# Batch 0's gate and up products as seven block products, and the weight sums for them spread over two slots

## The chip, the cores and the metric

The kernel runs on one core of one Trainium2 chip, in one launch. The metric is the device time of that launch in microseconds. Everything is float32. TensorE (PE) multiplies matrices into PSUM, VectorE (DVE), ScalarE (ACT) and GpSimd (POOL) work elementwise, and SyncE (SP) issues nearly all of the transfers, one after the other in program order; each engine likewise takes its own instructions in program order.

## The reference

One layer of a transformer: attention with a residual, then a gated feed-forward network with a residual, on four batches of 512 tokens of 512 features.

```python
B, T, D, FF = 4, 512, 512, 1376          # 32 heads of 16, 8 key/value heads

def attention(x):                         # x: layernorm of the input
    q, k, v = x @ Wq, x @ Wk, x @ Wv      # heads of 16; q and k are rotated (rope)
    att = einsum('bhgqd,bhkd->bhgqk', q, k) / sqrt(16)
    probs = softmax(where(causal, att, -inf))
    return (probs @ v) @ Wo

def ffn(x):                               # x: layernorm of the sum so far
    up = x @ W_up.T                       # 512 -> 1376
    gate = silu(x @ W_gate.T)             # 512 -> 1376
    return (gate * up) @ W_down.T         # 1376 -> 512

x = x + attention(layernorm(x))
x = x + ffn(layernorm(x))
```

## The kernel before

**Slots.** Attention goes by groups: a batch has eight, each with four of the 32 heads. A call of slot(b) works off the eight groups of batch b, and weaves other PE work between their scores as filler: a list of steps, each with a planned cost in microseconds. After each of the four score visits of a group, and in slots 1 to 3 after its averages too, gap(n) issues filler until a planned share of the slot's total is done. So the order on each engine is written out by the program and fixed. Slot 0 weaves in the projections (queries, keys, values) of batches 1 to 3; slot 1 the rest of batch 3's queries, batch 0's output projection, its second layernorm, all its gate and up products, the last 96 features (edge) and half of its down product; slots 2 and 3 the same kind of work for batches 1 and 2, and batch 3's feed-forward network comes after the last slot. By the planned costs slot 1 holds 123.0 us of filler and slot 2 117.8.

**A group on the engines.** PE makes scores in two orientations (L993, L1006) into two pairs of banks. DVE reads one for the row maxima (L1039), ACT takes the exponentials of the other (L1094) into tiles e0, e1 and e2, POOL masks these (L1099), and PE averages the values with them (L1121). At a group's end POOL also makes a masked copy of the queries for a later group (masked, L978); SP stores the maxima (lowest, L1080) and lays them into those query tiles (L1089, L1091) a group ahead. DVE transposes the averages (L1135), takes the reciprocal (L1138), and POOL scales them (L1145). While slot 0 runs, POOL also does half of the rotation of queries and keys (L359, L363) and spreads the keys (L425).

**Gate and up, two ways.** For batch 0, ordinary(n) takes ten blocks of 128 features, for each a gate half and an up half of four products over 512 tokens. Each product is issued as four column tiles of 32 (L299, while narrow is set), and the trace has two records of each tile. The weights of a block come by load_f from the inputs, two blocks ahead, into the tile shared. For batches 1 to 3, seven(b, n, blocks) takes ten units, each the gate or the up part of 256 features, as a 2x2 block product with seven multiplications instead of eight (Winograd's form). Its steps are a1, y1, y2, v1, v2, w1 and w2, each with two products over 256 tokens. DVE joins them (L738, L748, L749, L757), ACT copies one of them into the tail of the rotation table (once, L727), and POOL multiplies gate and up in slots 2 and 3 (L721). It reads four sums of the activations (sums_of, on DVE, L682), which lie in xnTs[1] under the name turn, and weight blocks that load_blocks brings from DRAM (packed, L675), about a unit ahead, in four kinds of places in the tile shared.

**The weight sums.** Of a unit's seven weight blocks, three are plain copies from DRAM to DRAM (copies, L653 and L654, issued in slot 0), and four are sums that POOL makes (packs, L640): two loads of 256 KB into half of a spare tile, four adds of 128x256, one store of 512 KB (L643). Before the change this spare tile is xnTs[1], and all ten units are made in slot 1, woven in by timed at planned times 8.2 us apart. Batch 0 cannot use them, and does not.

**Other queues.** The output weights (wo_sb) are loaded at the very start. The list idle holds POOL work that pool_steps issues a few at a time in each gap; before the change it is empty in slots 0 and 1. A load whose place was just stored from waits on SP until the store has landed, and whatever SP has to issue after it waits too.

Of the kernel before, what the change touches and what calls it, by code (L numbers as in the profile page):

```python
# [74 lines left out]
def preln_block_kernel(  # L75
# [87 lines left out]
    whole = NF - 1  # L163
    packed = [dram.tile([P, 7, 2 * P], F32, name=f"packed{u}") for u in range(whole)]
    turn = xnTs[1].rearrange("p k t -> p (k t)")
    sums = turn.rearrange("p (s k t) -> p s k t", s=4, k=2)
    spare = turn.rearrange("p (u f m) -> p u f m", u=2, f=4)
    rest_w = rope_sb[:, : 2 * NK * 96].rearrange("p (a k m) -> p a k m", a=2, k=NK)


# [4 lines left out]
    def load_w(t, src):  # L175
        nc.sync.dma_start(out=t, in_=src.rearrange("(k p) m -> p k m", p=P))
# [105 lines left out]
    idle = deque()  # L282

    def pool_steps(n):
        for _ in range(min(n, len(idle))):
            idle.popleft()[1]()

    def need(tag):
        while any(t == tag for t, _ in idle):
            pool_steps(1)  # L290
# [328 lines left out]
    def after(step):  # L619
        return 0.0, step  # L620

    def packs(u):


        w, at = (wg, wu)[u % 2], 2 * P * (u // 2)
        t = spare[:, u % 2]

        def load():
            for i in range(2):
                load_w(t[:, 2 * i : 2 * i + 2, :].rearrange("p f (k m) -> p (f k) m", k=2), w[:, at + P - P * i :][:, :P])  # L630

        def combine(n):
            a11, a12, a21, a22 = (t[:, f, :] for f in range(4))
            out_, one, two, op = (
                (a22, a21, a22, ALU.add),
                (a21, a11, a21, ALU.subtract),
                (a11, a22, a11, ALU.subtract),
                (a12, a12, a11, ALU.subtract),
            )[n]
            nc.gpsimd.tensor_tensor(out_, one, two, op)  # L640

        def store():
            nc.sync.dma_start(out=packed[u][:, 3:, :], in_=t)  # L643

        return load, combine, store
# [22 lines left out]
        )  # L668

    def load_blocks(kind, v):  # L670
        if v >= (B - 1) * whole:
            return
        blocks = places[kind][1]
        src = packed[v % whole][:, blocks[0] : blocks[-1] + 1 : max(blocks[-1] - blocks[0], 1), :]
        nc.sync.dma_start(out=place(kind, v).rearrange("p f k m -> p f (k m)"), in_=src)  # L675
# [8 lines left out]
    def seven(b, n, blocks):  # L684
# [16 lines left out]
            return t.rearrange("p (h t) -> p h t", h=2)  # L701

        def unit(u):
            v, a, f = (b - 1) * whole + u, u % 2, 2 * (u // 2)
            left, right = slice(0, 2 * P), slice(2 * P, T)
            out = (u_sb if a else home[:, f : f + 2, :]).rearrange("p f t -> p (f t)")
            corners = out.rearrange("p (h t) -> p h t", h=4)[:, 0:4:3, :]
            ps = {}

            def twice(t):  # L710
                return t.unsqueeze(1).broadcast_to([P, 2, 2 * P])

            def ended():
                for which in (1, 0):
                    g, t = home[:, f + which, :], u_sb[:, which, :]
                    if a == 0:
                        nc.scalar.activation(t, g, AF.Tanh, scale=0.5)
                        carried.append(lambda g=g, t=t: nc.vector.scalar_tensor_tensor(g, t, 1.0, g, ALU.add, ALU.mult))
                    else:
                        engine = nc.gpsimd if narrow[0] else nc.vector  # L720
                        engine.tensor_tensor(g, g, t, ALU.mult)  # L721

            def a1():
                load_blocks("y", v + 1)
                ps["a"] = bank()
                product(ps["a"][:, left], 1, place("a", v)[:, 0])
                nc.scalar.copy(once, ps["a"][:, left])  # L727

            def y1():
                load_blocks("v", v + 1)  # L730
                load_blocks("a", v + 1)
                ps["y"] = bank()
                product(ps["y"][:, left], 2, place("y", v)[:, 0])
                owed()

            def y2():
                product(ps["y"][:, right], 6, place("y", v)[:, 1])
                nc.vector.tensor_tensor(halved(out[:, T:]), halved(ps["y"]), twice(once), ALU.add)  # L738

            def v1():  # L740
                load_blocks("w", v + 1)
                ps["v"] = bank()
                product(ps["v"][:, left], 7, place("v", v)[:, 0])
                owed()

            def v2():
                product(ps["v"][:, right], 5, place("v", v)[:, 1])
                nc.vector.tensor_tensor(corners, halved(ps["v"]), twice(out[:, 3 * T // 2 :]), ALU.add)  # L748
                nc.vector.tensor_tensor(out[:, right], ps["v"][:, right], out[:, left], ALU.add)  # L749

            def w1():
                ps["w"] = bank()
                product(ps["w"][:, left], 4, place("w", v)[:, 0])

            def w2():
                product(ps["w"][:, right], 3, place("w", v)[:, 1])
                nc.vector.tensor_tensor(corners, halved(ps["w"]), corners, ALU.add)  # L757
                ended()

            return [(0.86, step) for step in (a1, y1, y2, v1, v2, w1, w2)]  # L760

        steps = []
        for u in range(whole):
            steps += unit(u)
            if u % 2:
                steps.append(after(lambda p=u // 2: later_sums(b, n, p, (0, 1))))
        t = [after(lambda s=s: sums_of(s)) for s in range(4)]
        ends = edge(n)
        steps[12:12] = [after(moved)]
        for cut, step in zip((44, 50, 56, 62, 66, 72), blocks):  # L770
            steps.insert(cut, after(step))
# [407 lines left out]
    begin1[1]()  # L1179
    load_w(wv_sb, wv)  # L1180
    load_columns(wq_sb, wq, P, D)
    load_w(wo_sb, wo)
    thin[0] = False
    for cost, step in turned:
        step()
# [53 lines left out]
    def slot(b, steps):  # L1239
# [19 lines left out]
        def gap(n):  # L1259
            nonlocal done, part  # L1260
            part += total * shares[n] / 8
            pool_steps((3, 2, 2, 0, 3)[n])
            done = fill(steps, part, done)

        for g in groups:
# [48 lines left out]
    early = [*rest1[16:-8], *turns, begin3, *rest2, *turned3, *rest3[:-24]]  # L1314
    for u in range(whole):
        early.insert(4 * u + 4, after(lambda u=u: copies(u)))
    slot(0, early)

    before, behind = attended(0, by_pe=(2, 3))
    tiles = list(down(0, 0))  # L1320
# [13 lines left out]
        assert not asides  # L1334
        return out_steps

    asides = []
    for u in range(whole):
        load, combine, store = packs(u)
        at = 8.2 * u + 6.0  # L1340
        asides += [(max(at - 9.9, 0.5), load), (at + 5.0, store)]
        asides += [(at + 1.0 * n, lambda n=n, combine=combine: combine(n)) for n in range(4)]
    asides += [(6.0, spilled), (34.0, load_down), (34.1, load_rest)]
    start1 = [
        before[0],
        *rest3[-24:-12],
        *before[1:],
        after(lambda: load_f(0)),
        *rest3[-12:-1],
        *behind,  # L1350
        rest3[-1],
        after(lambda: load_f(1)),
    ]
    blocks = [after(lambda kind=kind: load_blocks(kind, 0)) for kind in "ayvw"]
    layer = [*ordinary(0), *edge(0), *tiles[:5], *blocks, *tiles[5:cut]]
    slot(1, [*start1, *timed(layer, asides)])

    def split(b, n):

# [65 lines left out]
```

## Time and profile before

| | |
|---|---|
| time, median of 3 runs | 847.11 us (846.38 to 848.0) |
| the profiled execution | 848.06 us |
| its span, first to last instruction | 845.8 us |
| PE busy | 822.5 us, 97% |
| DVE busy | 545.5 us, 65% |
| POOL busy | 352.5 us, 42% |
| ACT busy | 231.3 us, 27% |
| moved by DMA | 101.57 MB, mean 120 GB/s |
| granted TensorE clock | 1.00 |
| stretch before slot 0 | 0 to 49.8 us |
| stretch after slot 3 | 705.0 to 845.8 us |

The times are from the first to the last instruction of the span. Busy times are unions: two matmuls that run side by side on different tiles of the array count once. A group of instructions has one line: source line, engine, operation, output and inputs by name, shapes, count, then its busy time, the mean of one, and the idle time of the engine just before its instructions with what ended most of it. Matmul ends are modelled, so a busy PE may still wait a little inside.

By the chain that ended last, PE is 76% of the span, DVE 12%, POOL 4% and DMA 3%. The filler's matmuls (L299 and L296) are 52% of it and the scores L993 12%.

### The profile page before, as it was taken

Reading aid. Unit: us, or ns where it says so; the run is one execution under the profiler, and the core shown is the slowest. Engines: PE = TensorE matmul, PEld = TensorE weight load, DVE = VectorE, ACT = ScalarE, POOL = GpSimd, SP = SyncE. Lnnn points to the kernel's source line nnn. Section 1 sums busy time; section 2 is a strip of 40 time slices with the busy share of each in tenths; the row PEclk is TensorE's granted clock in tenths of the full one; section 3 lists DMA queues with packets and bytes.
Section 4 is the critical chain, followed back from the end, with each engine's and each line's share of the span. In section 5 each row is a group of like instructions: output and inputs, shape, how many; then the busy total and the mean of one; then the engine's idle time right before and its main releaser. Section 6 shows DMA issues by size and latency. Waiting matters only on the chain.

```text
span 845.8 us, 28256 instructions
## 1 busy us (share of the span) xinstructions
PE 822.5 (97%) x11980; PEld 452.2 (53%) x11980; DVE 545.5 (65%) x1601; ACT 231.3 (27%) x342; POOL 352.5 (42%) x514
## 2 busy tenths in 40 slices
PE   6999999999999999999999999999999999999998
PEld 5654444544333335333555555436655556788887
DVE  7877777778555554458677776686877633656632
ACT  1045654422232322222233232222323331011100
POOL 4575574773544344223265634532244444101130
PEclk9999999999999999999999999999999999999999
DMA  8533304003764742253344632325333534545811
GB/s 259 124 96 78 91 16 91 5 3 64 232 191 144 235 137 77 88 200 77 84 155 140 196 115 66 115 47 151 96 97 103 162 106 148 119 146 174 291 33 50
DMA packets 149517, 101.57 MB, mean 120 GB/s; under 512 B 59696, under 2 KB 137264, under 8 KB 149136
## 3 DMA queue, kind: packets, MB, share of 16 engines
q1 hardware_dynamic: 149104, 94.01, 38.3%
q10 hardware_dynamic: 288, 5.77, 1.8%
q8 instruction: 94, 1.54, 0.8%
q14 instruction: 31, 0.25, 0.1%
HBM read 78.32 MB, written 25.17 MB: 122 GB/s over the span
## 4 chain that ended last, share of the span: by engine, by line
PE 76%; DVE 12%; POOL 4%; DMA 3%; issue 2%; ACT 1%; SPq 1%; POOLq 0%; DVEq 0%; ACTq 0%
PE mm L299 38%; PE mm L296 14%; PE sc L993 12%; DVE junk L1039 6%; PE av L1121 6%; PE sc L1006 4%; PE mm L590 2%; POOL e L1099 1%; DMA shared<-packed 1%; PE mm L582 1%; DVE st L218 1%; DVE rot L358 1%; ACT e L1094 1%; POOL home L425 1%; POOL qa L978 1%
## 5 line engine op out<-in xcount | busy, mean ns | idle before, releaser
L1039 DVE CUSTOM_DVE_ANT_0 junk<-sc,mask 128x128 f32<-128x128 f32 (+3 forms) x512 | 251.2, 491 | 139.0 <-PE sc L1006 78.4
L1094 ACT ACTIVATE e<-sc 128x1024 f32<-128x1024 f32 (+1 forms) x192 | 165.5, 882 | 384.4 <-PE sc L1006 300.7
L299 PE MATMUL mm<-xnT,shared 128*32 128x256 f32 (+1 forms) x3520 | 244.2, 420 | 2.3 <-DMA shared<-in_wg 1.5
L1099 POOL TENSOR_SCALAR_AFFINE_SELECT e<-e 128x512 f32<-128x512 f32 (+2 forms) x192 | 105.7, 560 | 225.4 <-ACT e L1094 222.3
L299 PEld LDWEIGHTS mm<-xnT,shared 128*32 128x32 f32 x3520 | 116.9, 110 | 113.0 <-issue 62.8
L993 PE MATMUL sc<-home,qa 32*64 32x512 f32 (+6 forms) x2048 | 156.1, 421 | 6.5 <-DVE low L1039 3.0
L1006 PE MATMUL sc<-qa,home 32*64 32x512 f32 (+6 forms) x2048 | 152.2, 427 | 1.5 <-DVE low L1039 0.8
L993 PEld LDWEIGHTS sc<-home,qa 32*64 32x64 f32 x2048 | 66.8, 131 | 90.2 <-DVE low L1039 29.1
L1121 PE MATMUL av<-e,home 128*32 128x512 f32 (+3 forms) x1024 | 81.9, 438 | 1.8 <-POOL e L1099 1.6
L296 PE MATMUL mm<-xnT,shared 128*128 128x256 f32 x360 | 80.3, 383 | 1.0 <-DMA shared<-packed 1.0
L296 PEld LDWEIGHTS mm<-xnT,shared 128*128 128x128 f32 x360 | 68.3, 192 | 12.8 <-issue 2.2
L299 PE MATMUL mm<-wd_sb,home 128*32 128x256 f32 (+3 forms) x848 | 71.4, 470 | 0.0
L1006 PEld LDWEIGHTS sc<-qa,home 32*64 32x64 f32 x2048 | 58.8, 130 | 22.5 <-issue 8.7
L1121 PEld LDWEIGHTS av<-e,home 128*32 128x32 f32 x1024 | 30.5, 109 | 47.2 <-issue 35.0
L299 PEld LDWEIGHTS mm<-wd_sb,home 128*32 128x32 f32 (+1 forms) x848 | 28.2, 110 | 36.9 <-issue 28.2
L299 PE MATMUL mm<-wo_sb,cx 128*32 128x512 f32 x384 | 45.4, 595 | 0.0
L797 POOL TENSOR_TENSOR wd_sb<-home 128x256 f32<-128x256 f32 x15 | 11.4, 759 | 75.6 <-DVE home L721 75.3
L1039 DVE DVE_READ_ACCUMULATOR2_ANT low<- 128x1 f32 x512 | 42.4, 83 | 0.0
L221 POOL TENSOR_TENSOR rstd<-rstd,neghalf 128x1 f32<-128x1 f32 x24 | 16.0, 667 | 56.8 <-DVE rstd L220 56.7
L1145 POOL TENSOR_TENSOR inv<-us,inverse 128x256 f32<-128x256 f32 x32 | 20.9, 654 | 44.5 <-DVE inverse L1138 44.3
L359 POOL TENSOR_TENSOR rot<-rot,rope_sb 128x512 f32<-128x512 f32 x18 | 25.7, 1425 | 23.0 <-DVE rot L358 22.8
L721 POOL TENSOR_TENSOR home<-home,u 128x512 f32<-128x512 f32 x20 | 25.2, 1281 | 21.2 <-DVE u L757 21.2
(146 smaller groups left out, 855.6 us busy)
## 6 DMA issues: line engine op xcount, KB each, us to landing
shared<-packed SPq DMA_DIRECT2D x90, 256.0 KB
flip<-u SPq DMA_DIRECT2D x88, 64.0 KB
packed<-xnT SPq DMA_DIRECT2D x10, 512.0 KB
xnT<-flip SPq DMA_DIRECT2D x18, 256.0 KB
wd_sb<-differences SPq DMA_DIRECT2D x7, 640.0 KB
shared<-packed SPq DMA_DIRECT2D x30, 128.0 KB
rows<-in_x SPq DMA_DIRECT2D x14, 256.0 KB
out<-rows SPq DMA_DIRECT2D x13, 256.0 KB
```

Of the source, the lines that this page charges most:

```text
L296: nc.tensor.matmul(out, lhsT=lhsT, rhs=rhs, start=start, stop=stop)
L299: nc.tensor.matmul(out[c : c + 32], lhsT=lhsT[:, c : c + 32], rhs=rhs, start=start, stop=stop)
L359: put(lambda: engine.tensor_tensor(rot, rot, sin, ALU.mult))
L590: nc.tensor.matmul(ps[96:P, ts(q, P)], lhsT=rest_w[:, a, kq, 32 * q : 32 * q + 32], rhs=xnTs[0][:, kq, most:], start=kq == 0, stop=kq == N ...
L721: engine.tensor_tensor(g, g, t, ALU.mult)
L993: nc.tensor.matmul(dst[at : at + 64, :n], lhsT=qa[g][rows_of(r), q : q + 64], rhs=keys_of(g)[rows_of(r), :n], start=True, stop=True,)
L1006: nc.tensor.matmul(dst[at : at + 64, first_q:], lhsT=keys_of(g)[rows_of(r), k : k + 64], rhs=qa[g][rows_of(r), P * j + first_q :], start=True,
L1039: nc.vector.tensor_tensor_reduce(out=junk[:, :n], in0=src, in1=mask[:, T - n : T] if i else mask[:, T:], scale=-1.0, scalar=BIG, op0=ALU.a ...
L1094: nc.scalar.activation(dst, src, AF.Exp, scale=1.0 / math.sqrt(DH))
L1099: nc.gpsimd.affine_select(out=e[rows, heads, c : c + P], in_=e[rows, heads, c : c + P], compare_op=ALU.is_ge, fill=0.0, base=base, pattern ...
L1121: nc.tensor.matmul(av[32 * r : 32 * r + 32, P * j :], lhsT=v[:, j, 4 * (m // 2) + r, DH * (1 - hf) : DH * (3 - hf)], rhs=e[:, r, c : c + n ...
L1145: nc.gpsimd.tensor_tensor(us[m][:, :, hf, :], turned[0][:, :, hf, :], by, ALU.mult)
```

## The change

Four things change together. (1) Batch 0's gate and up products go through seven instead of ordinary; its four activation sums stand at the head of its list, two before the steps a1 and y1 and two behind them, the edge comes at the end, and no sums for a seven-product down projection are queued. (2) The weight sums are made earlier: units 0 to 4 in slot 0, with the tile of the output weights as their spare, and units 5 to 9 in slot 1, with home tile 0's blocks 6 to 9 as theirs, which hold batch 0's keys and values until slot 0 ends and hidden features of batch 0 from unit 6 on. (3) They go through idle: one sum in each of the first three gaps of a group in slot 0, five a group in slot 1; a load or store that stands at the head of the list is issued along with them. (4) The output weights are loaded when slot 0's steps are done and the last sum is stored. The first blocks of kinds a and y are loaded at the start of slot 1, v and w behind the last of batch 3's queries.

```diff
-    spare = turn.rearrange("p (u f m) -> p u f m", u=2, f=4)
+    spares = (wo_sb.rearrange("p k t -> p (k t)"), homes[0][:, 6:10, :].rearrange("p f t -> p (f t)"))
+    spares = [t.rearrange("p (u f m) -> p u f m", u=2, f=4) for t in spares]
...
     def pool_steps(n):
-        for _ in range(min(n, len(idle))):
-            idle.popleft()[1]()
+        while idle and (n > 0 or idle[0][0] == "load"):
+            tag, step = idle.popleft()
+            n -= tag != "load"
+            step()
...
-        t = spare[:, u % 2]
+        t = spares[u // 5][:, u % 5 % 2]
...
     def load_blocks(kind, v):
-        if v >= (B - 1) * whole:
+        if v >= B * whole:
             return
...
         def unit(u):
-            v, a, f = (b - 1) * whole + u, u % 2, 2 * (u // 2)
+            v, a, f = b * whole + u, u % 2, 2 * (u // 2)
...
             steps += unit(u)
-            if u % 2:
+            if u % 2 and b > 0:
                 steps.append(after(lambda p=u // 2: later_sums(b, n, p, (0, 1))))
         t = [after(lambda s=s: sums_of(s)) for s in range(4)]
         ends = edge(n)
+        if b == 0:
+            return [t[0], t[1], *steps[:2], t[2], t[3], *steps[2:], *ends]
...
     load_columns(wq_sb, wq, P, D)
-    load_w(wo_sb, wo)
...
-            pool_steps((3, 2, 2, 0, 3)[n])
+            pool_steps(((1, 1, 1, 0, 0), (1, 1, 1, 0, 2), *[(3, 2, 2, 0, 3)] * 2)[b][n])
             done = fill(steps, part, done)
...
-    slot(0, early)
+
+    def pack(us):
+        made = [packs(u) for u in us]
+        idle.extend(("load", load) for load, _, _ in made[:2])
+        for at, (_, combine, _) in enumerate(made):
+            for n in range(4):
+                idle.append(("sum", lambda n=n, combine=combine: combine(n)))
+                if at and n == 1:
+                    idle.append(("load", made[at - 1][2]))
+                if at and n == 3 and at + 1 < len(made):
+                    idle.append(("load", made[at + 1][0]))
+        idle.append(("load", made[-1][2]))
+
+    def load_out():
+        need("sum")
+        pool_steps(0)
+        load_w(wo_sb, wo)
+
+    early.insert(4, after(lambda: pack(range(5))))
+    slot(0, [*early, after(load_out)])
...
-    asides = []
-    for u in range(whole):
-        load, combine, store = packs(u)
-        at = 8.2 * u + 6.0
-        asides += [(max(at - 9.9, 0.5), load), (at + 5.0, store)]
-        asides += [(at + 1.0 * n, lambda n=n, combine=combine: combine(n)) for n in range(4)]
-    asides += [(6.0, spilled), (34.0, load_down), (34.1, load_rest)]
+    blocks = [after(lambda kind=kind: load_blocks(kind, 0)) for kind in "ayvw"]
     start1 = [
         before[0],
+        *blocks[:2],
+        after(lambda: pack(range(5, whole))),
         *rest3[-24:-12],
         *before[1:],
-        after(lambda: load_f(0)),
         *rest3[-12:-1],
         *behind,
         rest3[-1],
-        after(lambda: load_f(1)),
+        *blocks[2:],
     ]
-    blocks = [after(lambda kind=kind: load_blocks(kind, 0)) for kind in "ayvw"]
-    layer = [*ordinary(0), *edge(0), *tiles[:5], *blocks, *tiles[5:cut]]
-    slot(1, [*start1, *timed(layer, asides)])
+    asides = [(6.0, spilled), (34.0, load_down), (34.1, load_rest)]
+    slot(1, [*start1, *timed([*seven(0, 0, ()), *tiles[:cut]], asides)])
```

## The prediction

> **What bounds the kernel now.** I read the page's busy line first: PE 822.5 us of 845.8, 97%, every other engine at most 65%. An average says nothing of one stage, so I asked for the busy times by stretch. Its borders are where the PE timeline has the first scores after the averages of groups 7, 15 and 23, that is the four slots.
>
> ```profile
> core 0: us, PE busy (x) PEld busy (x) DVE busy (x) ACT busy (x) POOL busy (x), PEclk, DMA share, GB/s
> ...
> 49.80:173.60 123.80, 116.62 (x2322) 57.96 (x2321) 90.88 (x319) 66.06 (x107) 80.46 (x117) 1.00 0.25 62
> 173.60:355.20 181.60, 179.68 (x2500) 69.71 (x2504) 105.61 (x345) 48.43 (x60) 81.65 (x120) 1.00 0.46 136
> 355.20:533.50 178.30, 176.62 (x3054) 88.59 (x3050) 125.10 (x371) 50.49 (x69) 74.85 (x108) 1.00 0.41 127
> ```
>
> Slot 1, where batch 0's gate and up products are, is PE alone: 179.68 of 181.60 us. Slot 0, which gets half of the weight sums, is 7.2 us short of full, and the reason is a POOL chain. Two views of one group's end there, POOL's timeline and then PE's (start, duration, instruction, idle time before it and what ended it):
>
> ```profile
> 101.66 1.27 POOL L363 TENSOR_TENSOR home<-home,rot 128x512 f32<-128x512 f32 x1
> 102.89 0.63 POOL L1099 TENSOR_SCALAR_AFFINE_SELECT e<-e 128x512 f32<-128x512 f32 x1
> ...
> 105.53 1.28 POOL L359 TENSOR_TENSOR rot<-rot,rope_sb 128x512 f32<-128x512 f32 x1 [0.67 <-DVE rot L358]
> 107.12 1.92 POOL L1099 TENSOR_SCALAR_AFFINE_SELECT e<-e 128x512 f32<-128x512 f32 x3 [0.31 <-ACT e L1094]
> 109.72 0.83 POOL L1099 TENSOR_SCALAR_AFFINE_SELECT e<-e 128x256 f32<-128x256 f32 x2 [0.68 <-ACT e L1094]
> 110.65 0.70 POOL L978 TENSOR_SCALAR qa<-home,rope_sb 128x512 f32<-128x512 f32 x1
> ```
> ```profile
> 108.80 2.43 PE L1121 MATMUL av<-e,home 128*32 128x512 f32 x32
> 111.40 0.64 PE L993 MATMUL sc<-home,qa 32*64 32x512 f32 x2 [0.17 <-POOL qa L978]
> ```
>
> PE begins the next group when POOL's masked query (L978) ends, and that stands behind the two e2 masks. So in slot 0 POOL's margin is only what it idles before those masks: here 0.67, 0.31 and 0.68 us.
>
> **Products, the term that pays.** Removed: 20 halves x 4 products over 512 columns. Added: 10 units x 7 products x 2 over 256 columns. Both prices are rows of the groups by shape, the first from slot 1, the second from slot 2, which runs exactly such 10 units beside the same attention work:
>
> ```profile
> L299 PE MATMUL mm<-xnT,shared 128*32 128x512 f32 x640 | 73.9, 595 | 1.5 <-DMA shared<-in_wg 1.5
> ...
> L299 PE MATMUL mm<-xnT,shared 128*32 128x256 f32 x1120 | 65.8, 381 | 0.8 <-DMA shared<-packed 0.5 <-DVE low L1039 0.3
> ```
>
> 73.9 - 65.8 = **8.1 us less**. Bounds: by whole slots the planner's costs for slots 1 and 2 differ by 5.2 us (123.0 against 117.8) and the spans by 3.3, so its own 8.6 for this exchange may be worth 6.7; slot 3's row (65.2) gives 8.7.
>
> A rule speaks against this: the Trainium skill (TensorE: Matmul & The Clock Gate, Part 3, The mechanism) says that a weight load overlaps matmuls in flight only if it goes to another row group, and these tiles all use every row. By that rule the 480 more loads, at the trace's 110 ns each, would stand 53 us on the path and turn the gain into a loss. The row decides: all 1120 loads lie in slot 2's group, and it is still 65.8.
>
> **The first wait of the layer.** Today PE waits 1.46 us at 213.63 for the first weights; the chain that ended last has the load as a piece of its own:
>
> ```profile
> 208.71 4.78 DMA shared<-in_wg
> ```
> ```profile
> 213.63 1.92 PE L299 MATMUL mm<-xnT,shared 128*32 128x512 f32 x16 [1.46 <-DMA shared<-in_wg]
> ...
> 218.60 3.70 PE L299 MATMUL mm<-xnT,shared 128*32 128x512 f32 x32
> ```
>
> The new first blocks a and y are loaded at the slot's start into places that are free, so **1.5 us** goes. But two waits come. In the instruction order as built, the layer starts after group 9's averages (today 218.60): products a1 and y1 take 2 x 0.87, so y2 is wanted at 220.3. It needs the second activation sum. On DVE, where today's transposition of the averages starts at 219.37, stand that (0.67), the reciprocal (0.26) and two sums (0.68 each in slot 2): ready at 221.8, a wait of 1.5. Behind it on DVE are two more sums and the next maxima, which the next scores' banks need; v1 and its fellows (2.6 us) cover those. Then v1: its block is issued on SP after the lowest values (219.47 + 0.34) and two pack loads (0.5 each), at 220.9. The nearest row, the 4.78 above, lands it at 225.7; with 512 KB of pack loads and 256 KB of its own at the 291 GB/s of the page's fullest slice and 1.4 us for a bare transfer (lowest to its landing) it is 4.0, 224.9. Wanted: y2 done 222.7 plus the scores' 1.0 = 223.7. I take 1.2. Sum **2.8 us**; bounds 0 (both land in time, as in slots 2 and 3, where edge work stands between) and 3.5.
>
> **The moved sums.** A sum is a 128x256 add on POOL:
>
> ```profile
> L640 POOL TENSOR_TENSOR xnT<-xnT x40: 722/732/742, 222.0 to 342.8; 128x256 f32<-128x256 f32 x40
> ```
>
> 0.73 plus 0.08 to the next: 0.81. Twenty leave slot 1 (16.2 us of POOL, no gain: PE was not waiting for it), and there ten gated products by 1.28 us come instead (L721's row of slot 2). Twenty enter slot 0: one to three ahead of each group's last masks. Against POOL's idle time there, group by group (counted from 0): in groups 1, 2, 5 and 7 they fit (before the masks POOL idles 3.6 us in group 2, 4.3 in 5). Groups 0 and 4 have one sum behind the four key spreads (L425) with no idle left: 0.81 each. Groups 3 and 6 have three: 2.43 less the 1.66 above = 0.77, and 2.43 less 1.75 = 0.68. Sum **3.1 us** on the path. Bounds: 0, if the masks still come in time, and all 16.2.
>
> The skill adds (GPSIMD Engine Reference, Key points) that POOL shares its SBUF interfaces with VectorE and contends with instructions of two SBUF inputs. The trace shows it for L359, 1.80 us beside DVE's L362 and else 1.28; at 0.5 for each of 20 sums that would be 10 us more POOL time. The forty sums' own 722 to 742 ns beside the same DVE show none, so I add nothing.
>
> **At nothing, and what hides them.** DVE in slot 1 grows from 105.6 towards slot 2's 125.1, ACT by about 2; slot 2 bears both with PE idle 1.7. SP: 20 weight loads (0.5 us each to issue) go, 40 block loads come; 10 pack loads and 5 stores move to slot 0 past the lowest values, query rows and batch 3's flips. Those query rows are needed a whole group (15 us) after issue, and a load that waits for a store holds SP 4.6 us at the longest today. The output weights (1 MB) leave the start, where PE runs without a break from 11 to 41 us, so nothing is gained; they are now issued after group 7, near 174.5, and land near 180 by the rate above, for a first use at 182.4. If that cover fails it costs its lateness, 0 to 2 us. In slot 1 the last pack store precedes the blocks of unit 6; POOL's last sum frees SP some 5 us after group 11, the blocks land some 6 later, wanted at about 12. Tight; 0 taken, 1 as bound.
>
> **Sum.** -8.1 - 1.5 + 2.8 + 3.1 = **-3.7 us**. The profiled execution took 848.06 (span 845.8, 2.3 around it), so 844.4 in its terms; the median of the runs, 847.11, is 0.95 lower: **843.4 us**.
>
> **Rivals.**
> *All hidden*: the sums fit POOL's 43 us of idle in slot 0 and the layer starts without waits: -8.1 - 1.5 = -9.6, 837.5. For it: POOL is at 65% there. Against: the 0.17 us waits for L978 in nearly every group; the margin is local.
> *Given back*: the products bring 6.7, the start costs 3.5, the output weights and unit 6 come late by 3, the sums cost their 3.1: -6.7 - 1.5 + 3.5 + 3 + 3.1 = +1.4, 848.5; with any one of them milder, no change. For it: four tight landings.
> *Slower*: POOL in slot 0 becomes the bound. Everything else stands at -6.8, so it decides from 6.8 / 0.81, more than 8.4 of the 20 sums on the path (I count 3.8). Twelve give 9.7 and 850.0, all give 16.2 and 856.5. For it: mask and query close every group on POOL. Against: the masks there waited 16.9 us for ACT's exponentials.
> *That it doesn't do what it says*: the built order of PE shows 560 narrow products in slot 1 where 320 wide ones stood; I give it nothing.
>
> **Numbers.** Forecast 0.50 (own range 841 to 846), all hidden 0.17, given back 0.17, slower 0.16. A change under 0.2%, 1.7 us, is no change here: 845.4 to 848.8. Faster: 0.45 of the forecast and 0.17, so 0.62; same: 0.05 and nearly all of the third, 0.21; slower 0.17. The range, 838.5 to 850.0, leaves out the best of the second case and the worse half of the last.
>
> **What would show it.** Right: slot 1 near 175 us (-8.1 - 1.5 + 2.8 from 181.6), its xnT,shared group near 66 us; slot 0 near 127 with longer waits for L978 in groups 0, 3, 4 and 6 only; in slot 1 a wait for DVE's sum, then one for a packed block, both once. Wrong: slot 0 longer by over 7, waits for packed blocks all through slot 1, or a change of slot 2 or 3.

## The result, and the profile after

The changed kernel takes **849.96 us** (median of 20 runs, 847.3 to 852.91), the kernel before 847.67 (20 runs beside them, 846.38 to 850.84): ratio 1.0024 with the 95% interval 1.0012 to 1.0035. By the ratio that is 2.0 us slower, where 3.7 us faster was forecast. The profiled execution took 849.87 us, its span is 848.0.

First the busy times by stretch, as before. The first line is slot 0. The second is cut where the same instruction stands in both kernels, from the averages of group 7 to those of group 16, so that it holds all of slot 1's work.

```profile
core 0: us, PE busy (x) PEld busy (x) DVE busy (x) ACT busy (x) POOL busy (x), PEclk, DMA share, GB/s
49.80:177.00 127.20, 118.36 (x2321) 57.78 (x2320) 91.97 (x318) 66.08 (x107) 94.63 (x138) 1.00 0.38 101
...
174.90:376.80 201.90, 196.25 (x3280) 93.38 (x3272) 139.77 (x419) 56.35 (x76) 86.43 (x120) 0.99 0.45 142
```

The same second cut of the kernel before:

```profile
171.10:375.20 204.10, 202.12 (x2804) 77.20 (x2799) 117.70 (x385) 53.62 (x66) 87.09 (x130) 1.00 0.46 142
```

Slot 0 is 3.4 us longer than before (127.20 against 123.80; 3.5 from its first averages to its last), near the 3.1 of the forecast. Slot 1 is only 2.2 us shorter, where 6.8 was forecast, though PE works 5.9 us less in it. PE now waits there for 5.6 us where it waited 2.0, and its clock is 0.99 and not 1.00. The profile has three places for this.

**The start of the layer.** PE's timeline (start, duration, instruction, idle time before it and what ended it), then DVE's and POOL's in the same microseconds:

```profile
219.55 1.99 PE L302 MATMUL mm<-xnT,shared 128*32 128x256 f32 x32
224.03 1.52 PE L302 MATMUL mm<-xnT,shared 128*32 128x256 f32 x16 [2.48 <-DVE xnT L685]
225.48 1.12 PE L998 MATMUL sc<-home,qa 32*64 32x512 f32 x2
...
227.42 3.02 PE L302 MATMUL mm<-xnT,shared 128*32 128x256 f32 x48
230.37 0.65 PE L998 MATMUL sc<-home,qa 32*64 32x512 f32 x2
```
```profile
221.20 1.75 DVE L685 TENSOR_TENSOR xnT<-xnT 128x512 f32<-128x512 f32 x1
222.98 0.99 DVE L685 TENSOR_TENSOR xnT<-xnT,xnT 128x512 f32<-128x512 f32 x1
223.90 1.21 DVE L685 TENSOR_TENSOR xnT<-xnT 128x512 f32<-128x512 f32 x1
225.03 0.68 DVE L685 TENSOR_TENSOR xnT<-xnT,xnT 128x512 f32<-128x512 f32 x1
```
```profile
219.78 1.28 POOL L362 TENSOR_TENSOR rot<-rot,rope_sb 128x512 f32<-128x512 f32 x1
221.14 1.26 POOL L366 TENSOR_TENSOR wd_sb<-wd_sb,rot 128x512 f32<-128x512 f32 x1
222.36 1.07 POOL L1150 TENSOR_TENSOR inv<-us,inverse 128x256 f32<-128x256 f32 x1
223.39 1.17 POOL L643 TENSOR_TENSOR home<-home 128x256 f32<-128x256 f32 x1
```

The products a1 and y1 run at 219.55, and y2 waits 2.48 us for the second activation sum. DVE began the sums 1.65 us behind the layer's start (221.20), as the forecast had it (1.7); but the first two took 1.75 and 0.99 us where slot 2's first two take 0.68. Each of the three slow sums began while an operation of POOL was under way and ended 0.54 or 0.55 us behind that operation's end (222.95 behind 222.40, 223.97 behind 223.43, 225.11 behind 224.56); the fourth, beside none, takes 0.68. POOL's scaling and weight sum, which began during the first and the second sum, are longer too (1.07 where the scaling took 0.62, 1.17 where the weight sum took 0.73). So the two engines took turns here. The kernel before has this already: slot 2's fourth sum, DVE first and then POOL, ends 0.55 us behind a mask.

```profile
417.74 1.13 DVE L682 TENSOR_TENSOR xnT<-xnT,xnT 128x512 f32<-128x512 f32 x1
417.69 0.63 POOL L1099 TENSOR_SCALAR_AFFINE_SELECT e<-e 64x512 f32<-64x512 f32 x1
```

Behind the wait, the two scores take 1.12 us where the same two take 0.65 at 230.37: the granted clock was cut to half. Busy times by stretch show it (columns as above, the clock is the third number from the end):

```profile
222.00:226.00 4.00, 1.97 (x24) 0.80 (x32) 3.97 (x5) 0.00 (x0) 2.81 (x4) 0.81 0.81 217
226.00:230.00 4.00, 4.00 (x60) 1.44 (x48) 2.73 (x7) 1.03 (x1) 1.20 (x2) 0.76 0.82 289
...
224.52:227.92 3.40, 3.40 (x36) 0.75 (x32) 2.19 (x4) 0.25 (x1) 1.49 (x3) 0.50 1.01 314
```

**A block in mid-layer.** PE's timeline, then the DMA issues of SP's queue:

```profile
292.10 1.07 PE L302 MATMUL mm<-xnT,shared 128*32 128x256 f32 x16 [1.88 <-DMA shared<-packed]
```
```profile
275.48 0.42 SPq L177 DMA_DIRECT2D wd_sb<-in_wd  x1
...
277.04 0.54 SPq L177 DMA_DIRECT2D rope_sb<-in_wg  x1
277.62 3.09 SPq L177 DMA_DIRECT2D rope_sb<-in_wu  x1
280.82 5.57 SPq L678 DMA_DIRECT2D shared<-packed  x4
```

The blocks of unit 7 are issued from 280.82 on, behind the 2.5 MB of the down weights and the edge weights, and their four issues take 5.57 us, the first alone 3.20. Over these 3.20 us the DMA engines' busy share is 1.03. The kernel before issued the same bulk loads at the same planned cost, but its weights came two blocks ahead. The step that waits is the unit's first, a1. The kernel's `place` gives block a one place in the tile shared, and y, v and w two each, so block a can't be loaded before a1 of the unit ahead has read its place.

**Slot 0.** The borders (first score behind the averages) move by +0.6, 0, 0, +1.7, +0.7, 0, +0.5 and 0 us in groups 0 to 7: the four groups the forecast named, and no other. Group 3, POOL's timeline, to be held against the one in the prediction:

```profile
107.81 0.74 POOL L643 TENSOR_TENSOR wo_sb<-wo_sb 128x256 f32<-128x256 f32 x1 [1.31 <-DMA wo_sb<-in_wg]
108.50 1.27 POOL L362 TENSOR_TENSOR rot<-rot,rope_sb 128x512 f32<-128x512 f32 x1
109.73 0.74 POOL L643 TENSOR_TENSOR wo_sb<-wo_sb 128x256 f32<-128x256 f32 x1
110.42 2.75 POOL L1104 TENSOR_SCALAR_AFFINE_SELECT e<-e 128x512 f32<-128x512 f32 x5
113.27 0.69 POOL L983 TENSOR_SCALAR qa<-home,rope_sb 128x512 f32<-128x512 f32 x1
```

POOL does not idle before the masks any more; all five (x5) stand in one run behind the sums. The first sum in this view also waits 1.31 us for a load, which the forecast had not, so group 3 costs 1.7 and not 0.77.

### The profile page after: what moved, and what is told of

The parts are those of the page before. It is cut to its first block, busy times and chain, and to the rows that moved or that the text cites. A ratio compares the mean times of both kernels' runs of the same rounds, so it can differ in the third digit from the quotient of the medians.

```text
span 848.0 us, 29313 instructions
## 1 busy us (share of the span) xinstructions
PE 818.9 (97%) x12460; PEld 468.2 (55%) x12460; DVE 568.6 (67%) x1635; ACT 233.9 (28%) x352; POOL 366.1 (43%) x524
## 4 chain that ended last, share of the span: by engine, by line
PE 73%; DVE 12%; POOL 5%; DMA 3%; issue 3%; SPq 2%; ACT 1%; DVEq 0%; POOLq 0%; ACTq 0%
PE mm L302 35%; PE mm L299 14%; PE sc L998 11%; DVE junk L1044 6%; PE av L1126 5%; PE sc L1011 3%; DMA shared<-packed 2%; PE mm L593 2%; POOL e L1104 2%; PE mm L585 1%; DVE rot L361 1%; DVE st L219 1%; POOL rot L362 1%; ACT e L1099 1%; POOL qa L983 1%
## 5 line engine op out<-in xcount | busy, mean ns | idle before, releaser
L302 PE MATMUL mm<-xnT,shared 128*32 128x256 f32 x4000 | 237.3, 382 | 5.5 <-DMA shared<-packed 3.0
L302 PEld LDWEIGHTS mm<-xnT,shared 128*32 128x32 f32 x4000 | 133.1, 110 | 102.8 <-issue 33.5
L1126 PE MATMUL av<-e,home 128*32 128x512 f32 (+3 forms) x1024 | 84.3, 438 | 4.5 <-POOL e L1104 4.3
L724 POOL TENSOR_TENSOR home<-home,u 128x512 f32<-128x512 f32 x30 | 37.9, 1282 | 31.8 <-DVE u L760 31.8
L802 POOL TENSOR_TENSOR wd_sb<-home 128x256 f32<-128x256 f32 x15 | 11.4, 757 | 75.7 <-DVE home L724 75.4
L720 ACT ACTIVATE u<-home 128x512 f32<-128x512 f32 x40 | 23.0, 623 | 61.9 <-DVE home L760 52.7
```

Of the source, the lines that this page charges most:

```text
L302: nc.tensor.matmul(out[c : c + 32], lhsT=lhsT[:, c : c + 32], rhs=rhs, start=start, stop=stop)
L1126: nc.tensor.matmul(av[32 * r : 32 * r + 32, P * j :], lhsT=v[:, j, 4 * (m // 2) + r, DH * (1 - hf) : DH * (3 - hf)], rhs=e[:, r, c : c + n ...
```

## The experiments

All start from the changed kernel. Slot 0 is the time from the first averages of group 0 to those of group 7, slot 1 from those of group 7 to those of group 16, both in the profiled execution; the last column has the idles of PE of 1 us or more in slot 1. Each of the twelve was run 4 to 10 times, and its ratio is to the kernel before run beside it (medians of 847.42 to 849.13). The profiled execution lies within 1.0 us of the median in most rows, but 2.6 below it in run 1, 4.5 above in run 7, 1.4 above in run 8 and 2.8 above in run 9.

| kernel | median us | ratio to before, 95% interval | slot 0 | slot 1 | idles |
|---|---|---|---|---|---|
| before | 847.67 | 1 | 109.0 | 204.0 | 1.46 |
| changed | 849.96 | 1.0024 (1.0012 to 1.0035) | 112.5 | 201.9 | 2.48, 1.88 |
| 1 plain quarters | 851.16 | 1.0036 (1.0025 to 1.0048) | 112.3 | 201.4 | 3.48, 1.32 |
| 2 no sums in slot 0 | 847.50 | 0.9996 (0.9984 to 1.0009) | 108.7 | 203.8 | 2.48, 2.44 |
| 3 down weights in parts | 848.61 | 1.0007 (0.9997 to 1.0017) | 112.6 | 199.6 | 2.50 |
| 4 quiet POOL | 848.59 | 1.0005 (0.9995 to 1.0016) | 113.7 | 199.3 | 1.44, 1.41 |
| 5 early v and w | 849.60 | 1.0019 (1.0008 to 1.0030) | 112.6 | 201.9 | 2.49, 1.99 |
| 6 plain quarters, early v | 848.28 | 1.0003 (0.9990 to 1.0016) | 114.0 | 200.8 | 1.57, 1.55, 1.79 |
| 7 sums in holes | 851.38 | 1.0055 (1.0036 to 1.0073) | 115.3 | 206.9 | 2.00, 1.13, 2.95, 2.05 |
| 8 four repairs | 854.06 | 1.0075 (1.0057 to 1.0092) | 114.5 | 204.4 | 5.20 |
| 9 spill in parts | 846.59 | 0.9985 (0.9970 to 1.0001) | 114.0 | 200.3 | 2.68 |
| 10 all repairs | 844.24 | 0.9958 (0.9942 to 0.9974) | 109.1 | 199.7 | 2.28 |
| 11 holes without loads | 848.46 | 1.0002 (0.9986 to 1.0019) | 109.3 | 202.4 | 2.49, 1.90 |
| 12 later transfers | 841.58 | 0.9918 (0.9900 to 0.9936) | 109.4 | 197.1 | none |

### What slot 0 pays: 2, 7 and 11

**2, no sums in slot 0.**

```diff
         def combine(n):
...
-            nc.gpsimd.tensor_tensor(out_, one, two, op)
+            if u >= 5:
+                nc.gpsimd.tensor_tensor(out_, one, two, op)
```

> The changed kernel without the twenty POOL adds of units 0 to 4, which stand in slot 0; their loads and stores stay. (The weight blocks made of them are then wrong.) My theory: the 3.8 us by which slot 0 is longer than before are these adds standing ahead of the masks and the query copy in groups 0, 3, 4 and 6, one of them behind a late load; all of it goes, slot 0 is back at 107.9 to 108.2 us from the first to the eighth group's border (before: 107.95, changed: 110.83 plus 0.93 in front of it), and the time is 846. Rival, that the moved loads and stores (SP, DMA traffic) cost it: slot 0 stays 2 us or more above before.

Slot 0 is 108.7 us, 0.3 below the kernel before (109.0): the adds cost all of the 3.5 us, the moved loads and stores none. (The 3.8 of the expectations counts 0.3 us that lies ahead of the first averages.) The time falls less than slot 0 does, by 2.4 us if the ratios are compared: slot 1 grew by 2.0, where the block wait is now 2.44 us and a second stretch of half clock follows it.

**7, sums where POOL idles.** They go ahead of a group's first rotation, not into the gaps behind its visits.

```diff
-            pool_steps(((1, 1, 1, 0, 0), (1, 1, 1, 0, 2), *[(3, 2, 2, 0, 3)] * 2)[b][n])
+            pool_steps(((0, 2 * (g == 2), 0, 0, 0), (1, 1, 1, 0, 2), *[(3, 2, 2, 0, 3)] * 2)[b][n])
...
                 if thin[0]:
+                    pool_steps((0, 4, 2, 2, 2, 4, 2, 2)[g] if n == 0 else 0)
                     odd_steps((1.3, 0.95, 0.95, 1.05)[n], (2, 1, 1, 0)[n])
```

> The changed kernel with the twenty sums of slot 0 put where POOL is idle: right behind the scaling of the averages, before the group's first rotation (4 in group 1, 2 in groups 2, 3, 4, 6 and 7, 4 in group 5), and two more after group 2's second visit; none in group 0. Theory, that only sums ahead of a group's last masks cost time: slot 0 is as long as before, 3.8 us shorter, and the time 846. Rival, that POOL in slot 0 has no room and every sum costs in the end: at most 1 us goes.

Neither: 851.38, and in the profiled execution one group alone is 4.8 us longer than before the change, the others within 1.2. Group 5 in PE's, DVE's and SP's timelines:

```profile
144.22 1.16 PE L1011 MATMUL sc<-qa,home 32*64 32x256 f32 x16 [4.09 <-DVE low L1044]
```
```profile
141.72 0.71 DVE L317 STREAM_TRANSPOSE u<-xa 128x512 f32<-128x512 f32 x1 [4.53 <-DMA flip<-u]
```
```profile
132.02 0.38 SPq L646 DMA_DIRECT2D packed<-wo_sb  x1
134.70 0.94 SPq L177 DMA_DIRECT2D wo_sb<-in_wg  x2
135.73 3.24 SPq L321 DMA_DIRECT2D flip<-u  x4
```

With four sums at once, a store of sums (132.02) and the load into the same tile (134.70) come right behind each other. The load holds SP until the store has landed, the flips of batch 3 behind it are late, DVE waits 4.53 us for the tile they read, and PE waits 4.09 us for the maxima behind that on DVE.

**11, the same without a store and a load in one group** (2 sums in group 5, and the two left over in group 7).

```diff
-            pool_steps(((1, 1, 1, 0, 0), ...
+            pool_steps(((0, 2 * (g == 2) + (g == 7), g == 7, 0, 0), ...
...
+                    pool_steps((0, 4, 2, 2, 2, 2, 2, 2)[g] if n == 0 else 0)
```

> The changed kernel with only slot 0 altered, the sums placed as in the former. Theory, from the wait of 4.1 us for DVE in group 5 of the other placement (flips held up on SP behind a store and a load): without that, slot 0 is as long as before the change and all of 3.8 us is saved there; the start of slot 1 keeps its two waits: 846. Rival, that early sums in themselves hold DVE up (shared access to memory): slot 0 is 2 us or more longer than before, and 848 or more.

Slot 0 is 109.3, where it was 109.0 before the change: the theory, twenty sums for next to nothing. Group 3 on POOL:

```profile
100.03 1.55 POOL L643 TENSOR_TENSOR wo_sb<-wo_sb 128x256 f32<-128x256 f32 x2
...
107.45 1.29 POOL L362 TENSOR_TENSOR rot<-rot,rope_sb 128x512 f32<-128x512 f32 x1 [0.66 <-DVE rot L361]
109.05 1.92 POOL L1104 TENSOR_SCALAR_AFFINE_SELECT e<-e 128x512 f32<-128x512 f32 x3 [0.31 <-ACT e L1099]
111.65 0.83 POOL L1104 TENSOR_SCALAR_AFFINE_SELECT e<-e 128x256 f32<-128x256 f32 x2 [0.68 <-ACT e L1099]
```

The idle times of POOL before the rotation and the masks are 0.66, 0.31 and 0.68 us again, those of the kernel before: the two sums ran in the 1.6 us in which POOL waits for the first rotation's input. The median fell by 1.9 us (by the ratios) and not by 3.8. Eight of these ten runs show a mean clock of 0.998 or less; the other two took 845.8 and 846.0.

### What the start of slot 1 pays: 1, 4, 5 and 6

**1, plain quarters for the sums.**

```diff
+        if b == 0:
+            rights = (*rights[:3], *(x[:, 2 * j : 2 * j + 2, 256 * h : 256 * h + 256] for j, h in ((1, 0), (0, 1), (1, 1), (1, 1))))
```

> The changed kernel, with batch 0's products reading plain quarters of the activations in place of the four sums; DVE still makes the sums, so only PE's wait for them goes. (Batch 0's result is then not the layer's.) My theory: the 2.48 us idle before y2 at 224 us goes, and with it the stretch of 3.4 us at a granted clock of 0.5, worth about 1.7 us more; block v is then wanted some 2.5 us earlier and may cost up to 1.5 us. Slot 1 201.9 - 4.2 = 197.7 us, or 199.2 with that wait, between the averages of groups 7 and 16; the time 846 to 847.5. Rival, that the clock falls whatever PE waits for: a stretch at 0.5 stays and only 2.5 us go. Rival, that the narrow products themselves are dearer than the old row: less than 1 us goes.

It is no faster, 851.16; the last rival's number, but not for its reason. The wait for the sum went and a longer one came in its place, for block v; PE's timeline and SP's queue (in this execution slot 1 is 0.5 us shorter):

```profile
226.61 2.80 PE L302 MATMUL mm<-xnT,shared 128*32 128x256 f32 x48 [3.48 <-DMA shared<-packed]
```
```profile
220.49 1.71 SPq L177 DMA_DIRECT2D home<-in_wu  x2
222.24 2.48 SPq L678 DMA_DIRECT2D shared<-packed  x5
```

Block v is issued at 222.24 behind two pack loads of 0.85 us each (0.5 in the forecast), is wanted at 223.1 and lands at about 226.6. In the changed kernel the wait for the sum covered it. The profiled execution was at full clock behind its 3.48 us; the other seven of the eight runs show a mean clock of 0.998 or less.

**4, POOL quiet beside the first sums.**

```diff
-            engine = nc.vector if early and m == 0 else nc.gpsimd
+            engine = nc.vector if early and m == 0 else None if (b, m) == (3, 3) else nc.gpsimd
...
+            if engine:
+                put(lambda: engine.tensor_tensor(rot, rot, sin, ALU.mult))
...
+            pool_steps({(9, 4): 0, (10, 0): 0, (10, 1): 2, (10, 4): 4}.get((g, n), now))
```

> The changed kernel with POOL kept quiet beside the first activation sums: the two POOL operations of the last query rotation of batch 3 are left out, and the three weight sums that follow group 9's averages come a group later. (Batch 3's last queries are then not rotated in full.) My theory: the sums took 1.75 and 0.99 us because POOL's two-input operations ran beside them; they take 0.68 to 0.75 each now, y2 starts at about 222.7 instead of 224.0, the idle is 1.1 to 1.3 us, which is what the prediction had (1.5). If the half clock needs an idle of 2 us or more, it goes too, and slot 1 is 3.0 us shorter, 847; if it comes after any idle it stays, and slot 1 is 1.3 us shorter. Rival, that the sums are slow for a reason on DVE itself: they stay above 1.5 and 0.9 us and the idle at 2.4.

The views of PE, DVE and POOL:

```profile
226.40 1.07 PE L302 MATMUL mm<-xnT,shared 128*32 128x256 f32 x16 [1.44 <-DVE xnT L687]
```
```profile
224.63 0.69 DVE L687 TENSOR_TENSOR xnT<-xnT 128x512 f32<-128x512 f32 x1
225.36 0.99 DVE L687 TENSOR_TENSOR xnT<-xnT,xnT 128x512 f32<-128x512 f32 x1
```
```profile
224.79 1.01 POOL L1152 TENSOR_TENSOR inv<-us,inverse 128x256 f32<-128x256 f32 x1 [1.55 <-DVE inverse L1145]
```

The first sum is back at 0.69: it began ahead of the one POOL operation left there, and that operation took 1.01 us instead. The second sum began behind it, at 225.36, and takes 0.99, up to 0.55 us behind its end at 225.80. So the slow sums are POOL's doing, by what POOL has begun when a sum comes. The wait is 1.44 us, nearly the 1.5 of the prediction though the second sum is still 0.3 too long, no half clock follows in this execution, and slot 1 is 2.5 us shorter. Three of ten runs show a mean clock of 0.998 or less, against 14 of 20 of the changed kernel.

**5, blocks v and w early**, and **6, both.**

```diff
-        *rest3[-12:-1],
+        *rest3[-12:-3],
+        blocks[2],
+        *rest3[-3:-1],
+        blocks[3],
         *behind,
         rest3[-1],
-        *blocks[2:],
```

> The changed kernel with the first blocks v and w loaded as soon as the parts of the query weights that lie in their places have had their last product (v behind the fourth last step of batch 3's last queries, w behind the second last), at about 214 us instead of 222.6. Theory, formed on the first experiment, that the start of slot 1 has two waits side by side (the activation sum until 224.0, block v until about 226.6), of which the later-wanted one is covered by the other: nothing changes, the wait for the sum stays at 2.4 to 2.5 us and the time at 849.5 to 850. Rival, that the late blocks are what the start costs and the sum is only the first to show: 2 us or more go.

> Both covers taken away: products of batch 0 on plain quarters instead of the sums (which DVE still makes; batch 0's result is then not the layer's), and blocks v and w loaded early. Theory of the two waits: PE runs through the start without an idle of over 0.6 us, the granted clock stays at 1.00 there, and against the first experiment (idle 3.48 us for block v) 3.5 us or more go: 845 to 846.5. Rival, a third cover behind the two (DVE's maxima, held up by four sums, free the score banks late): an idle of 1 us or more at the scores that follow, and 847 or more.

5 came out as the theory of two waits has it: 849.6, the wait for the sum still 2.49. In 6 the 3.48 us are gone too and the clock stays at 1.00, but the time is 848.28, not 845 to 846.5, and the rival with a third cover is right in part:

```profile
228.66 0.64 PE L1000 MATMUL sc<-home,qa 32*64 32x512 f32 x2 [1.57 <-DVE low L1046]
```

In DVE's timeline the maxima (227.19 to 228.60) stand behind the four sums, which end at 226.66, and the score banks came free late. A second idle, 1.55 us at 243.19 in the midst of a row of scores, has no releaser in the profile; it falls while the spill fills the DMA engines, and more than that was not shown.

### The block loads: 3, 8, 9, 10 and 12

**3, the down weights in parts** (load_part(f) loads the rows of one feature block).

```diff
...
-    asides = [(6.0, spilled), (34.0, load_down), (34.1, load_rest)]
+    asides = [(6.0, spilled), (34.1, load_rest)]
+    asides += [(22.0 + 3.0 * f, lambda f=f: load_part(f)) for f in range(NF)]
```

> The changed kernel with the 2.5 MB load of the down weights split into eleven loads, 3 us of planned filler apart, from 22 on (in one piece at 34 before). My theory: unit blocks no longer stand behind 2.5 MB, the 1.88 us idle of PE at 292 us (for a packed block) goes, and nothing else changes: the time is 848. Rival, that the block was late for another reason, the 384-byte packets of the edge weights or SP's queue: the wait stays at 1 us or more, and the time at 849.5 to 850.

848.61, as expected; no idle of over 0.6 us is left near 292, and slot 1 is 2.2 us shorter.

**8, four repairs**: 3, 5, 7, and the first two sums ahead of the last query step.

```diff
         *behind,
+        *layer[:2],
         rest3[-1],
```

> Four repairs together: sums of slot 0 in POOL's idle time, first blocks v and w early, the first two activation sums right behind the transposes (ahead of the last query step, the maxima and POOL's last rotation), the down weights in eleven pieces. By my theory the three things that ate the gain go: 3.8 in slot 0, 2.5 of waiting and 1.7 of half clock at slot 1's start, 1.9 at 292 us, together 9.9: from 850.0 to 840, which is 7.5 below the kernel before, its products' 8.1 less what small waits remain. If the products are worth only 6.7, it is 841.5; if the waits come back in another place, 843 or more.

854.06, the slowest of all. The waits at the start are gone, and those of group 5 (as in 7) and a new one stand in their place: PE, SP's queue, and the DMA engines from 222 to 254 us (busy tenths in 40 slices of 0.8 us):

```profile
247.25 2.36 PE L302 MATMUL mm<-xnT,shared 128*32 128x256 f32 x20 [5.20 <-DMA shared<-packed]
```
```profile
238.72 10.85 SPq L678 DMA_DIRECT2D shared<-packed  x4
```
```profile
DMA  0000000289988179899999899899599996150000
```

Four block issues take 10.85 us, the first alone 5.66; the fourth comes only at 249.24, when PE is running again. From 235 us on the spill of batch 3's queries (2.8 MB in one piece) shares the DMA engines with them, and these are full (a busy share of 1.02 over the first issue). The earlier PE is there, the more of this it sees: behind the sum, block v and the maxima it was the next cover.

**9, the spill in parts too** (spill_part(f) stores one block; slot 0 as in the changed kernel, the rest of the repairs as in 8), and **10, with slot 0 as in 11.**

```diff
+    asides += [(10.0 + 2.5 * f, lambda f=f: spill_part(f)) for f in range(NF)]
```

> The changed kernel with the start of slot 1 repaired: blocks v and w early, the first two activation sums right behind the transposes, the down weights in eleven pieces, and the spill of batch 3's queries (2.8 MB, in one piece from 235 us on) in eleven pieces too, 2.5 us of planned filler apart from 10 on; slot 0 as in the changed kernel. Theory, formed on the wait of 5.2 us at 247 in the kernel with four repairs: behind the sum and block v stands a third cover, the block loads that share the DMA engines with the spill (all busy from 236 to 244 us). With it gone too, no idle of PE over 1 us is left in slot 1, the clock stays at 1.00, and 2.5 + 1.7 + 1.9 = 6.1 us go from the 850.0: 844. Rival, that the blocks come late because SP waits for stores of sums and for PE's reads, not for bandwidth: 3 us or more of waiting for packed blocks stay near 245 us, and 847 or more.

> The same repairs of slot 1, and in slot 0 the sums in POOL's idle time, but without a store and a load in one group where batch 3's flips are issued (2 in group 5 instead of 4; 2 in each group's idle time after the averages, 4 in group 1, two more after visits of groups 2 and 7). Theory: 3.8 us more than the former go: 840, 7.5 below the kernel before. If the slot has no room for them after all, 842 to 844.

In both the start has no idle over 0.5 us. Where the bulk pieces meet, near 280 us, a block wait of 2.68 and 2.28 us came back, in both at step a1 of unit 6, so 9 reached 846.59 and 10 reached 844.24, not 844 and 840. The wait of 5.20 us in run 8 is at a1 of unit 2.

**12, the bulk transfers later**: spill from 14 on, down weights from 46 on, edge weights at 46.

> The kernel with all repairs, its remaining wait aimed at: 2.3 us at 276 us for a packed block, where pieces of the spill, pieces of the down weights, the edge weights and a store of sums lie on the DMA engines at once. The spill's pieces go from 14 on, 2.8 us of planned filler apart, the down weights from 46 on, 2.2 apart, the edge weights at 46 (10, 22 and 34 before); the DMA engines are nearly idle after 304 us. Theory, that block loads are late only where bulk transfers fill the DMA engines: no wait of 1 us or more for a packed block is left in slot 1, and 2.3 us go, 842. Rival, that SP's order (a store waiting for POOL, blocks behind it) makes them late: a wait of 2 us stays, 844.

841.58 us, 0.9918 of the kernel before (0.9900 to 0.9936): the version that beats both. PE's waits of 171 to 372 us (total, times, longest), and the busy times of slot 1:

```profile
PE av L1126 <- POOL e L1104: 1.1, 2, 0.6
PE mm L302 <- DMA shared<-packed: 0.4, 1, 0.4
```
```profile
171.90:369.00 197.10, 195.09 (x3280) 94.23 (x3272) 137.23 (x419) 56.15 (x76) 87.15 (x121) 1.00 0.46 148
```

The theory came out: no wait of 1 us or more is left, and the longest for a packed block is 0.4 us, at a1 of unit 1. With the same products, sums and bytes as the changed kernel, only in another order and in smaller transfers, slot 1 is 7.0 us shorter than before the change and PE works 7.0 us less in it. Every wait of 0.3 us or more for a packed block behind unit 0 of slot 1, in all of these kernels, is at a step a1; whether a second place for block a would have served as well was not tried.

## Why the prediction was wrong

The forecast was 3.7 us faster, the result 2.0 us slower. In the profiled executions the miss is 5.5 us (849.87 against 844.4), and it can be laid out by the terms of the sum (us, plus is slower):

| term of the sum | forecast | measured | from |
|---|---|---|---|
| products | -8.1 | -7.0 | PE busy in slot 1, 202.12 before, 195.09 in run 12 |
| first wait of the layer | -1.5 | -1.5 | no wait for in_wg is left |
| start of seven | +2.8 | +2.5 | the idle at 224 us |
| half clock behind it | none | +1.2 | PE busy 196.25 against 195.09 of run 12, the same work |
| blocks in mid-layer | 0 | +1.9 | the idle at 292 us |
| averages waiting for masks in slot 1 | none | +0.8 | waits for POOL's e, 1.1 against 0.2 |
| moved sums in slot 0 | +3.1 | +3.5 | 112.5 against 109.0 |
| elsewhere | 0 | +0.6 | start +0.3, slot 2 +0.3, after slot 3 +0.4, around the span -0.4 |
| sum | -3.7 | +2.0 | the two profiled executions differ by 1.8, so 0.2 is left over |

**Products**: right in kind, mis-sized. The rows of the products differ by 7.6 us (73.9 before, 77.7 less the 11.4 of other products in run 12), all of PE by 7.0. The prediction's bound of 6.7, from the planner's costs, was nearer than its 8.1 from the row of slot 2; where the 0.6 us between 7.6 and 7.0 stands was not traced.

**"At nothing"** is the step that failed outright: it put the issue and the landing of the forty block loads at no cost. It asked of SP whether units 5 and 6 and the output weights would land, and these did. It did not ask what stands ahead of block loads that now run all through slot 1: the down weights (1.9 us, gone in run 3), and, hidden in this kernel but laid bare in run 8, the spill. Nor did it hold where the DMA engines were full that a load costs 0.5 us to issue: one block load took 3.20 us behind the down weights and one 5.66 beside the spill. The same passage put POOL and ACT in slot 1 at nothing, and the averages wait 0.8 us more for masks there. Ahead of the first of the two waits POOL works almost without a break from 191.00 to 198.1 us, a weight sum among it; ahead of the second POOL itself waits 2.47 us for ACT.

**The start of seven** had the right two waits and a size of 2.8 for the two (its own terms, 1.5 and 1.2, add up to 2.7); the first alone was 2.5, and what it set off is not a wait at all but the clock, 1.2 us more. PE is busy in slot 1 for 196.1 to 196.5 us in the four executions with one stretch at half clock there (changed, 3, 5, 11), and for 194.7 to 195.5 in the six with none (1, 4, 6, 9, 10, 12). "So I add nothing" was wrong for DVE: the prediction weighed the Trainium skill's rule (GPSIMD Engine Reference, Key points), that POOL and VectorE contend where VectorE has two SBUF inputs, by what POOL's forty sums took, and looked at the wrong side. The sums on DVE are the two-input instructions, and they grew from 0.68 to 1.75, 0.99 and 1.21 us; run 4 shows the first back at 0.69 with POOL quiet ahead of it. There the wait is 1.44 us, near the forecast's 1.5, in part by luck, as the second sum still took 0.99.

**Block v** came neither "once" nor visibly: the wait for the sum covered it, and run 5, which loads it early, gains nothing. Run 1 uncovers it (3.48 us).

**The moved sums** were right in place and nearly in size; group 3's wait for a load, 1.31 us, is the part that was not foreseen.

Of the rivals, *given back* (848.5) was the nearest in its terms, with 6.7 for the products, 3.5 for the start and 3.1 for the sums against 7.0, 3.7 and 3.5. That its total came so near is luck: its last term, 3 us for output weights and unit 6, did not come, and another of its size did, the blocks behind the down weights and the masks, 2.7. *Slower* had the number (850.0, with twelve sums on the path) but not the reason, as slot 0 pays 3.5 us and not 9.7. *All hidden* was not out of the kernel's reach, only out of this order: run 12 gets 7.0 of its 9.6 us.

## What to carry to other kernels

Work that is cheap in sum is dear where it stands ahead of the last instruction of a stage; the same twenty sums cost 3.5 us behind the visits of a group and 0.3 in the idle time some microseconds earlier. Where an engine is at 97%, waits lie behind one another: removing the covered one gains nothing (run 5), and removing the one in front uncovers the next (runs 1, 6 and 8), so price a start by everything that must have arrived, and test repairs together as well as alone. When a stage goes from few large weight loads to many small ones just in time, look at every bulk transfer that shares its queue or the DMA engines, and move or split it first.

## What the runs showed of the hardware that was not expected

**The clock falls after short idles.** In the fourteen profiled executions (the one before among them), from slot 0 on, 24 idles of PE of 1.0 to 1.99 us had no stretch at a granted clock of 0.5 beside them; of 15 idles of 2.00 us or more, 11 had one that began within 1.7 us of their end, the shortest of the 11 being 2.05 us long. The four without were 2.00, 2.28, 2.68 and 3.48 us, so length alone does not decide it, and runs of one kernel differ in it. What else decides was not tested. The stretches lasted 3.41 or 6.83 us. One more, at 44.6 us in run 8, had no idle of 0.8 us near it. The Trainium skill (TensorE: Matmul & The Clock Gate, Part 1, What's actually happening) has a free-running window of 3413 ns, which the lengths agree with; its advice to avoid idles above about 3 us (Why this matters for your kernels) is too wide for this case, where 2.05 to 2.50 us were enough seven times.

**POOL and DVE take turns.** In the same executions DVE made 220 activation sums (subtractions of 128x512, both inputs in SBUF). Of these, 66 began while an operation of POOL was under way, one-input masks included, and 65 of them ended 0.54 to 0.55 us behind that operation's end, after 0.69 to 1.77 us; the other 154 took 0.63 to 0.69. The one exception (run 7) began 0.05 us behind POOL's rotation and took 0.63, and the rotation took 1.79 instead of 1.27. The other way round, POOL's two-input operations of 128x256 that began during such a sum took 0.94 to 1.07 us (scaling, else 0.62) and 1.17 to 1.19 (weight sum, else 0.73). So which of the two began first decided which one paid.
